# Pinning sixteen small loads in GpSimd's queue, in a two-layer graph network kernel

## The chip, the cores and the metric

The kernel runs on one core of one Trainium2 chip. The time is device microseconds of one launch. The core has five engines with a queue each: TensorE (PE in the profile, its weight loads PEld), VectorE (DVE), ScalarE (ACT), GpSimd (POOL) and SyncE (SP). GpSimd, SyncE and ScalarE also issue DMA transfers from their queues; the transfers themselves are done by 16 DMA engines that all queues share.

## What is computed

Two graph layers with residuals and layer norms over 4096 nodes with 512 features, with a dense 4096 x 4096 adjacency matrix. Cut to what matters:

```python
# layer 0
xw  = (x > 0) @ sign(L0_gnn_weight).T
x   = layernorm(x + relu(adj @ xw))
# layer 1
node_att = softmax(x @ node_w, axis=0)
h   = x @ edge_w
e   = where(adj > 0, h @ h.T, NEG_BIG)
out = (adj * node_att * softmax(e, axis=1)) @ (x @ weight) + bias
x   = layernorm(x + out)
```

The case is about layer 0's second half: the product with `adj`, and what is prepared there for layer 1.

## The kernel before

**Layer 0.** x and its products are cut into 32 blocks of 128 rows. For each block the kernel multiplies 32 tiles of 128 x 128 of the transposed adjacency matrix with `xw`, which lies in SBUF. To keep float32 accuracy[...], each adjacency tile is split into `hi` (a rounded copy, ScalarE, line 413) and `lo` (the rest, VectorE, line 415), and each part has its own matmul (lines 423 and 424). The split works in quarters of a block: eight tiles at a time, with two buffers each for `hi` and `lo`. A quarter is 16 matmuls, some 3.6 us of TensorE. The adjacency tiles (`at`) come through SyncE's queue, half a block a load, in three buffers. The first two rows of blocks (`early`) are multiplied while `xw` is still being made, so that after that stage the finishing work of two blocks comes at once.

**What follows a block.** `rest` is a Python generator, and one piece of it runs in each quarter of the blocks that follow, so that its instructions are spread between the splits:

- a first piece adds the residual and takes the row statistics (lines 320 to 322);
- a second normalises (line 326), and with `tensor_tensor_reduce` into the scratch tile `scr` takes the block's share of the node attention (line 327);
- a third adds the bias into `scr` (line 331) and stores it to `x1_d` in DRAM through GpSimd's queue (line 332). `scr` has one buffer;
- a fourth calls `left` after every second block, and starts `lefts` for some;
- a fifth transposes the block on TensorE (line 383), and `lefts` goes on in the pieces after it.

**Left operands for later.** The big products of layer 1 use a scheme with seven products instead of eight (Strassen's, in Winograd's form). Its left operands are sums and differences of pairs of blocks, and `left` makes them here: lines 371 to 374 on VectorE into `sums_l`, and four stores to `lop_d` in DRAM, all through GpSimd's queue (lines 375 to 378). For three of the seven operands the scheme is applied a second time within the operand. `lefts` makes these inner combinations, for the last two of every four pairs of blocks (eight times in all). It loads three pieces of an earlier pair's operands back from `lop_d` into the tile `low` with two loads (line 352), waits three pieces, and combines them with the present pair (lines 358 to 361: four operations of 128 x 128 for one operand, four of 128 x 256 for the other two). It stores the results to `lop2_d` (lines 363 and 364). `low` has one buffer.

**What else is in GpSimd's queue.** `premask` turns pieces of the adjacency matrix into masks for layer 1 (line 303 on VectorE), and stores them through GpSimd's queue (line 304). So in this stage the queue holds x1_d stores, lop_d stores, the `low` loads, lop2_d stores and mask stores, and a waiting instruction holds up all behind it.

**What sets the order.** The layer-0 loop runs under `tc.manual_schedule` for VectorE and ScalarE: their instructions keep the order of the program text. Those of GpSimd's queue do not: the scheduler of the language orders them by its own priorities and by when operands and buffers are ready in its reckoning. A DMA that reads what another wrote waits for that one's landing, and a load into `low` waits until the tile is free. `tc.keep_in_program_order(...)` around an instruction fixes its place among the instructions of its engine; `premask` uses it already for its conversion at line 303. The last block's `lefts` does not run in the loop: it is kept in `late` and goes on between the products of `hT`, the first product of layer 1 (line 101), where no manual schedule holds.

Of the kernel before, what the change touches and what calls it, by code (L numbers as in the profile page):

```python
# [29 lines left out]
def kernel(  # L30
# [13 lines left out]
    nc = tc.nc  # L44
# [114 lines left out]
    with (  # L159
# [153 lines left out]
        def rest(n, b, xb, acc, before):  # L313
# [3 lines left out]
            rstd = small.tile([P, 1], F32, name="rstd")  # L317
            scr = wp.tile([P, D], F32, name="scr", tag="scr")
            inner = n % 2 and n // 2 % BG > 1 and lefts(n // 2, xb)
            nc.vector.scalar_tensor_tensor(xb, acc, 0.0, xb, ALU.max, ALU.add)  # L320
            nc.vector.bn_stats(stats, xb)
# [25 lines left out]
        def lefts(b, high):  # L347

            to, of = lop2_d[b // BG][:, :, b % BG - 2], lop_d[b // BG][:, :, b % BG - 2, :]
            low = wp.tile([P, len(SPLIT), HD], F32, name="low")  # L350
            for k, m in ((slice(2), slice(4, 7, 2)), (2, 3)):
                nc.gpsimd.dma_start(low[:, k, :], of[:, m, :])
            for _ in range(3):
                yield
            for k, a, to_a in ((2, high[:, HD:], sums_l[:, 0, :]), (slice(2), sums_l[:, 1:4:2, :], None)):
                to_a = a if to_a is None else to_a
                (l11, l21), (l12, l22), (s4, s1) = ((x[..., :P], x[..., P:]) for x in (low[:, k, :], a, to_a))
                nc.vector.tensor_add(s1, l22, l21)
                nc.vector.tensor_sub(l21, l11, l21)
                nc.vector.tensor_sub(l11, s1, l11)  # L360
                nc.vector.tensor_sub(s4, l12, l11)
                yield
                nc.gpsimd.dma_start(to[:, k, :2], to_a.rearrange("p (n f) -> p n f" if k == 2 else "p k (n f) -> p k n f", f=P))
            nc.gpsimd.dma_start(to[:, :, 2:], low.rearrange("p k (n f) -> p k n f", f=P))
# [1260 lines left out]
```

## Time and profile before

| | before |
|---|---|
| median of 3 runs | 1927.56 us (1927.24 to 1929.25) |
| the profiled execution's own time | 1931.16 us |
| its span | 1929.4 us |
| TensorE busy in the span | 1908.7 us |
| mean granted TensorE clock | 0.997 |
| DMA | 520.93 MB, mean 270 GB/s |
| layer 0 | to about 516 us |
| `hT` products | 516 to 613 us |
| layer 1's attention and output | from 613 us |

The profile is of one execution, with instructions, waits and DMA packets recorded. Lines of its views name an engine, the source line (L352 is line 352), the operation, what it writes and reads ("low<-lop_d"), and idle time of the engine before it with what ended that ("<-DMA lop_d<-xb": the landing of the transfer from `xb` to `lop_d`). A transfer issued by GpSimd shows there as DMA_DIRECT2D, and its length there is that of the issue alone; when it landed is told apart. In a line of busy times by stage stand the stretch, its length, the busy time of PE, PEld, DVE, ACT and POOL with their instructions, the granted TensorE clock, the busy share of the DMA engines, and GB/s.

### The profile page before, as it was taken

To read this page: it belongs to the slowest core of one execution; us is meant where nothing else is said; L and a number is where in the kernel's file an instruction comes from. 1 tells how busy PE (TensorE), PEld (TensorE's weight loads), DVE (VectorE), ACT (ScalarE), POOL (GpSimd) and SP (SyncE) were. 2 spreads that over 40 slices of the span, in tenths; PEclk is the share of its full clock that TensorE was granted. 3 is DMA by queue.
4 is the path that set the end of the run, shared out by engine and by line. 5 is a ranking of instruction groups with operands and counts; after the bars stand their busy time and mean duration, and the time that the engine had idled before them with its cause. 6 is when DMAs were issued, how large, how long until landed. Compare 5 with 4: busy or idle time off the path is not lost.

```text
span 1929.4 us, 20429 instructions
## 1 busy us (share of the span) xinstructions
PE 1908.7 (99%) x6816; PEld 1224.0 (63%) x6816; DVE 1436.1 (74%) x2113; ACT 1023.3 (53%) x1647; POOL 309.5 (16%) x449
## 2 busy tenths in 40 slices
PE   8999999999999999999999999999999999999998
PEld 6788888888744445444555556666666666656646
DVE  6577777776876467566754877898779988888847
ACT  5333333333211477566767666656676567657731
POOL 0123232232331111101110111111111111110100
PEclk9999999999999999999999999999999999999999
DMA  9789989899585479477874888878777877787731
GB/s 306 274 297 341 337 316 353 303 346 329 204 285 196 157 268 336 165 256 276 305 277 161 305 292 305 288 287 287 265 287 277 296 276 278 263 290 257 286 118 55
DMA packets 143913, 520.93 MB, mean 270 GB/s; under 512 B 15040, under 2 KB 15040, under 8 KB 136128
## 3 DMA queue, kind: packets, MB, share of 16 engines
q1 hardware_dynamic: 64368, 235.43, 36.1%
q0 software_dynamic: 67632, 248.54, 34.1%
q10 hardware_dynamic: 11808, 35.66, 5.0%
q8 instruction: 54, 0.88, 0.2%
q14 instruction: 51, 0.42, 0.1%
HBM read 397.93 MB, written 121.63 MB: 269 GB/s over the span
## 4 chain that ended last, share of the span: by engine, by line
PE 93%; DVE 3%; DMA 2%; ACT 1%; issue 0%; ACTq 0%; POOL 0%; DVEq 0%
PE bank L1186 36%; PE seven L779 15%; PE acc L424 11%; PE acc L423 11%; PE pe L706 5%; PE seven L101 5%; PE po L1336 4%; PE pt L668 3%; PE acc L236 1%; PE acc L235 1%; PE pt L383 1%; PE pw L213 1%; DMA lop<-lop_d 1%; PE bank L1336 0%; DVE slot L955 0%
## 5 line engine op out<-in xcount | busy, mean ns | idle before, releaser
L1186 PE MATMUL bank<-lent,lop 128*128 128x256 f32 (+1 forms) x1496 | 483.1, 473 | 0.1
L1186 PEld LDWEIGHTS bank<-lent,lop 128*128 128x128 f32 x1496 | 284.2, 190 | 166.9 <-issue 140.1
L424 PE MATMUL acc<-xw,lo 128*128 128x512 f32 x960 | 376.0, 392 | 4.6 <-DVE lo L415 4.5
L423 PE MATMUL acc<-xw,hi 128*128 128x512 f32 x960 | 377.8, 394 | 0.0
L1186 PE MATMUL bank<-slot,lop 128*128 128x512 f32 (+1 forms) x800 | 288.1, 506 | 3.1 <-DMA lop<-lop_d 2.3
L413 ACT CAST hi<-at 128x1024 fp32r<-128x1024 f32 x120 | 126.3, 1052 | 211.0 <-PE acc L423 152.5
L1186 PEld LDWEIGHTS bank<-slot,lop 128*128 128x128 f32 x800 | 152.6, 191 | 118.0 <-issue 104.0
L1197 ACT COPY over<-bank 128x512 f32<-128x512 f32 x200 | 116.1, 584 | 202.3 <-PE bank L1186 198.5
L424 PEld LDWEIGHTS acc<-xw,lo 128*128 128x128 f32 x960 | 181.2, 189 | 42.2 <-DVE lo L415 5.2
L423 PEld LDWEIGHTS acc<-xw,hi 128*128 128x128 f32 x960 | 181.1, 189 | 37.0
L415 DVE TENSOR_TENSOR lo<-at,hi 128x1024 fp32r<-128x1024 f32 x120 | 147.0, 1225 | 68.8 <-ACT hi L413 68.3
L706 PE MATMUL pe<-hT 128*128 128x512 f32 (+3 forms) x384 | 132.1, 486 | 0.0
L639 ACT ACTIVATE line<-line,nmax_c 128x512 f32<-128x512 f32 x160 | 114.8, 725 | 22.6 <-DVE nmax_c L630 22.3
L630 DVE CUSTOM_DVE_ANT_0 line<-lent,slot 128x512 f32<-128x512 bf16 x140 | 90.7, 689 | 47.6 <-ACT slot L716 26.7
L1348 DVE SCALAR_TENSOR_TENSOR xb<-po,f,xb 128x256 f32<-128x256 f32 x84 | 40.3, 481 | 73.6 <-PE po L1336 73.6
L706 PEld LDWEIGHTS pe<-hT 128*128 128x128 f32 x384 | 64.6, 191 | 41.3 <-issue 33.8
L779 PE MATMUL seven<-hT 128*128 128x512 f32 x192 | 89.8, 593 | 0.0
L955 DVE CUSTOM_DVE_ANT_1 lent<-lent,line 128x2048 f32<-128x2048 f32 x39 | 88.7, 2284 | 0.0
L1159 ACT COPY bank<-over 128x512 f32<-128x512 f32 x144 | 86.7, 603 | 0.0
L668 PEld LDWEIGHTS pt<-ident,lent 128*128 128x128 f32 x418 | 52.3, 141 | 52.1 <-issue 38.6
L669 ACT COPY slot<-pt 128x512 f32<-128x512 f32 (+3 forms) x123 | 68.4, 559 | 23.2 <-PE pt L668 23.2
L958 ACT ACTIVATE lent<-lent 128x2048 f32<-128x2048 f32 x39 | 74.9, 1919 | 8.5 <-DVE lent L955 8.2
(270 smaller groups left out, 2947.9 us busy)
## 6 DMA issues: line engine op xcount, KB each, us to landing
lop<-lop_d SPq DMA_DIRECT2D x154, 512.0 KB, 4.6
at<-in_adj_t_dram SPq DMA_DIRECT2D x60, 1024.0 KB, 7.3
slot<-in_adj_t_dram POOLq DMA_DIRECT2D x39, 1024.0 KB, 7.8
lent<-s_d POOLq DMA_DIRECT2D x38, 1024.0 KB, 7.9
s_d<-slot POOLq DMA_DIRECT2D x30, 1024.0 KB, 7.3
lent<-in_adj_t_dram POOLq DMA_DIRECT2D x25, 1024.0 KB, 8.0
lent<-in_adj_dram SPq DMA_DIRECT2D x48, 512.0 KB, 5.3
s_d<-lent POOLq DMA_DIRECT2D x48, 512.0 KB, 4.3
```

The source lines that it names most:

```text
L101: nc.tensor.matmul(banks[bank][q], lop(m, q)[k], rop(m)[k], start=(first and k == 0), stop=(k == K - 1), skip_group_check=not first,)
L413: nc.scalar.copy(hi, aq)
L415: nc.vector.tensor_sub(lo, aq, hi.bitcast(F32))
L423: nc.tensor.matmul(acc, hi[:, c, :], xw[:, kb, :], start=(kb == 0), stop=False)
L424: nc.tensor.matmul(acc, lo[:, c, :], xw[:, kb, :], start=False, stop=(kb == NB - 1))
L630: nc.vector.tensor_tensor_reduce(line, mask, src, -1.0, HUGE, ALU.add, ALU.min, accum_out=nmax_c[:, b, c : c + 1])
L639: nc.scalar.activation(line, line, AF.Exp, bias=nmax_c[:, b, c : c + 1], scale=-1.0, accum_out=sum_c[:, b, c : c + 1])
L668: nc.tensor.transpose(pt[:, j, :], src[:, ts(j, P)], ident)
L706: nc.tensor.matmul(pe[:, lo * P :], hT[:, k, ts(A * BG + i, P)], hT[:, k, (B * BG + lo) * P : (B + 1) * W], start=(k == 0), stop=(k == KD ...
L779: nc.tensor.matmul(ps, left[m][:, k, q, :], right[m][:, k, :], start=(first and k == 0), stop=(k == KD // 2 - 1), skip_group_check=not first,)
L1186: nc.tensor.matmul(ps, lop[:, k, :], rop[:, k, :], start=start, stop=(k == K - 1), skip_group_check=True)
L1197: nc.scalar.copy(self.to(), self.bank[:, : self.w])
```

## The change

The two loads into `low` are wrapped in `tc.keep_in_program_order`:

```diff
             to, of = lop2_d[b // BG][:, :, b % BG - 2], lop_d[b // BG][:, :, b % BG - 2, :]
             low = wp.tile([P, len(SPLIT), HD], F32, name="low")
             for k, m in ((slice(2), slice(4, 7, 2)), (2, 3)):
-                nc.gpsimd.dma_start(low[:, k, :], of[:, m, :])
+                tc.keep_in_program_order(nc.gpsimd.dma_start(low[:, k, :], of[:, m, :]))
             for _ in range(3):
                 yield
```

In the program text `lefts` starts right after `left`. So each pair of loads now stands in GpSimd's queue directly behind the stores of lines 378 and 377 of the same pair of blocks. Before, the loads of the first of each two `lefts` stood some dozens of instructions earlier, between the stores of blocks before, and those of the second stood right behind the first's last stores. A piece of the start of GpSimd's queue, before and after:

```
before                          after
L376 lop_d<-xb                  L376 lop_d<-xb
L352 low<-lop_d                 L332 x1_d<-scr
L332 x1_d<-scr                  L378 lop_d<-sums_l
L378 lop_d<-sums_l              L377 lop_d<-sums_l
L377 lop_d<-sums_l              L375 lop_d<-xb
L375 lop_d<-xb                  L332 x1_d<-scr
L352 low<-lop_d                 L304 mask_d<-pair
L332 x1_d<-scr                  L304 mask_d<-pair
```

The other engines' orders stay the same but for VectorE's at the start of the `hT` products: there line 463, which prepares a right operand, now comes ahead of the last block's combinations at lines 358 to 361. Some of the work that follows them there (lines 122, 123, 303, 501 and 507) changes places by one or a few instructions.

## The prediction

> **What bounds the kernel now.** I read the page's busy shares first, then the busy time by stage, then who waited for whom in layer 0, and last the chain of work that ended last, followed through the one place where TensorE stood still.
>
> From the page (busy us, share of the span, instructions), and the busy time of each engine in two stretches of layer 0:
>
> ```profile
> PE 1908.7 (99%) x6816; PEld 1224.0 (63%) x6816; DVE 1436.1 (74%) x2113; ACT 1023.3 (53%) x1647; POOL 309.5 (16%) x449
> ...
> 60.00:100.00 40.00, 35.46 (x153) 28.88 (x152) 24.43 (x42) 11.91 (x17) 7.94 (x12) 0.91 0.71 240
> 100.00:500.00 400.00, 400.00 (x1815) 331.12 (x1814) 293.47 (x474) 129.92 (x159) 117.90 (x166) 1.00 0.90 328
> ```
>
> TensorE bounds the kernel. In 100 to 500 us, the bulk of layer 0, it is busy for all 400 us: whatever GpSimd waits for there costs nothing. Only 60 to 100 us has a hole, of 4.5 us, and a granted clock of 0.91. So the change can gain only there, and can lose anywhere. The waits of layer 0 (60 to 560 us: total us, times, longest):
>
> ```profile
> POOL low L352 <- DMA lop_d<-sums_l: 22.1, 4, 6.6
> POOL low L352 <- DMA lop_d<-low: 19.2, 4, 5.8
> POOL low L352 <- DMA lop_d<-xb: 13.8, 2, 7.2
> POOL low L352 <- issue: 13.7, 2, 7.1
> DVE scr L327 <- DMA x_d<-scr: 6.4, 3, 5.5
> PE acc L424 <- DVE lo L415: 4.5, 1, 4.5
> ```
>
> The 16 loads at L352 hold GpSimd's queue for 22.1 + 19.2 + 13.8 + 13.7 = 68.8 us in 12 waits. One of them, in the chain (start us, us, what), reaches TensorE:
>
> ```profile
> 69.02 7.71 DMA lop_d<-xb
> ...
> 77.00 0.57 POOL low L352
> 77.57 6.56 DMA x_d<-scr
> ...
> 84.96 1.15 DVE lo L415
> ...
> 86.15 0.79 PE acc L424
> 86.94 0.43 PE acc L423
> ```
>
> The load waited until the store of its own source had landed. The store x1_d<-scr, queued behind it, was held from 72.6 us (its L331 ended at 72.33; other such stores start 0.3 us after theirs) to 77.57. `scr` has one buffer, so VectorE's next L327 waited for that store, and the split `lo` stands behind L327. The timelines of VectorE and TensorE there (start, us, engine, instruction, idle before it and releaser):
>
> ```profile
> 78.17 0.55 DVE L326 TENSOR_SCALAR xb<-xb,mv,rstd 128x512 f32<-128x512 f32 x1
> 84.26 0.69 DVE L327 CUSTOM_DVE_ANT_0 scr<-xb,nw_b 128x512 f32<-128x512 f32 x1 [5.54 <-DMA x_d<-scr]
> ...
> 81.14 0.47 PE L423 MATMUL acc<-xw,hi 128*128 128x512 f32 x1
> 86.15 0.79 PE L424 MATMUL acc<-xw,lo 128*128 128x512 f32 x1 [4.54 <-DVE lo L415]
> 86.74 0.63 PE L423 MATMUL acc<-xw,hi 128*128 128x512 f32 x1
> ...
> 91.32 0.40 PE L424 MATMUL acc<-xw,lo 128*128 128x512 f32 x1
> ```
>
> [...] at 77.57 us the held store starts the moment the load has issued. [...] lop_d<-xb landed at 69.02 + 7.71 = 76.73 us, the load started at 77.00. [...] After the 4.54 us hole the records show 0.43 us from matmul to matmul, against 0.227 before it.
>
> **The change, part by part.** No instruction is added or removed: 16 loads move in GpSimd's queue, some of VectorE's work at the very end of layer 0 with them (4), and nothing on TensorE, ScalarE or SyncE. Before, the scheduler pulled them ahead. Pinned, each pair stands behind the L378 and L377 of its own block, where the source text has it.
>
> (1) The load at 77.00 goes from in front of the x1_d store. The store then issues at about 72.65. TensorE's loss, from 81.14 to 91.32 us: 10.18 us for 13 matmul steps, which at full pace take 0.32 (the step behind four transposes, as from 73.39 to 73.71) + 12 x 0.227 = 3.04. So 7.1 us: 4.7 of idleness and 2.4 of slow clock.
>
> What is late next? L327 could start at 78.75, when L326 is done. The store must land by then, 6.1 us after its issue. The 32 stores at L332 took 2.3 / 6.0 / 9.9 us (least, median, most). The one before it took 3.45, with spare DMA time: the share of the DMA engines is 0.25 to 0.36 in 74 to 78 us. It comes out of the queue behind lop_d<-xb (76.7), so I put it at 77 to 78. L327 (0.69) and `lo` (1.23) then end at 80.65, and TensorE wants `lo` at 81.46. The cover is 0.8 us: the store may take 6.9 us for nothing. At 9.9 it would land at 82.55 and leave 3.0 us of hole, most of it with the slow clock. The next loads of `at`, issued at 68.1 and 76.5, landed by 82.1, before the casts that want them even 7 us earlier. I take the full 7.1.
>
> (2) The other 11 waits of GpSimd go, 61 us of its queue. They are worth 0: TensorE has no hole in 100 to 500 us, and VectorE's other two waits for the store (0.26 and 0.59 us) reach nobody.
>
> (3) The loads come later, and VectorE's L358 may now wait for them. In the steady rhythm (block 2, times from L374 at 136.81) L378 issues 0.26 later and takes 1.02, L377 0.55, the pair 0.72 and 0.57. So the second load issues at +2.55, and L358 wants it at 146.96, which is +10.15: 7.6 us later.
>
> ```profile
> 146.96 0.29 DVE L358 TENSOR_TENSOR sums_l<-xb,low 128x128 f32<-128x128 f32 x1
> ...
> 149.40 1.23 DVE L415 TENSOR_TENSOR lo<-at,hi 128x1024 fp32r<-128x1024 f32 x1
> ```
>
> Behind L358 stand L359 to L361, L331, a mask conversion and this `lo`, which ends at 150.63; TensorE takes it up at 152.20. The slack is 1.57 us. So the load is free up to 9.15 us after its issue. Nearest rows: the loads themselves, 2.7 / 6.5 / 8.3 us, and L304, which holds that place in the queue now, in the loaded stretch of 400 to 430 us 7.9 / 8.4 / 11.0. [...] From above, 11.0 would be 1.85 us of TensorE in each of the 7 blocks inside the loop. I take 0, since both the median and the largest load fit.
>
> (4) The last block (15) is combined while layer 1's hT products run. Its loads now issue behind L377, which ended at 525.10: the second at about 525.8. Loads there took 2.7 to 3.1 us, so it lands near 529 instead of 520.6. VectorE's order changes with it: L463 is put ahead of L358. Eight small combinations (4 x 0.29 + 4 x 0.42 = 2.8 us) and L122 (0.69) then end near 532.6, and TensorE wants that bank at 533.91. It costs nothing with 1.3 us of cover; a landing of 8.3 us would cost about 4. GpSimd's reduction at L500 and the mask stores behind it shift by 1.3 us, with over 4 us before VectorE's use of the mask piece that waits for them (it landed at 540.8, used at 546.80).
>
> Sum against the profiled execution: 1931.16 (span 1929.4, 1.8 around it) - 7.1 = 1924.1. The runs' median lies 3.6 below the profiled execution, and I carry the saving over: 1927.56 - 7.1 = 1920.5.
>
> **Rivals.** A measurement of this kernel can tell 0.2%, 3.9 us, from no change.
> A, the full gain, 0.70: 1920.5. [...] DMA chance later in the kernel (a single 2.3 us wait for a lop load at 1719 us, with its own slow clock) adds about a microsecond each way: 1918.5 to 1922.5.
> B, the x1_d store still lands late, 0.12: at 8 to 9 us from issue 1.1 to 2.1 us of hole remain, some with slow clock, about 1924. For it: half the stores take over 6.0. Against: the idle DMA engines at 74 to 78 us.
> C, nothing gained, 0.08: the hole reopens at another wait behind it, 1927.5. Against: the chain shows no other wait within 4 us of that path.
> D, slower, 0.10: L358 waits for the pinned loads, with `lo` behind it. It decides from 9.15 us of landing, and must come to over 11 us to outweigh the gain by 3.9: 10.7 us at all 7 blocks. At 11.0 it is 7 x 1.85 = 13 us, 1927.56 - 7.1 + 13 = 1933.5. For it: DMA share 0.90 in this stretch and one L304 at 11.0. Against: no load over 8.3.
>
> The range takes in A and B, and leaves out C and D, 0.18: 1918.5 to 1926. Faster by over 0.2% is A and half of B: 0.76. Within it, the other half and C: 0.14. Slower: D, 0.10.
>
> **What would show it.** Right: L352 never starts after a DMA it waited for, L327's 5.54 us is gone, TensorE is full in 60 to 100 us with clock 1.00, and 100 to 500 stays at 400.00. Wrong: idle before L358 on "DMA low<-lop_d" over 1.6 us, a hole before L424 anywhere, or idle TensorE at 530 to 540 us.

## The result, and the profile after

| | before | after |
|---|---|---|
| median | 1927.88 us (6 runs, 1927.24 to 1929.82) | 1921.53 us (6 runs, 1920.88 to 1923.42) |
| profiled execution's own time | 1931.16 us | 1922.03 us |
| its span | 1929.4 us | 1920.3 us |
| first matmul at L423 to first `hT` matmul (L101) | 457.48 us | 450.33 us |

The ratio is 0.9966, 95% interval 0.9953 to 0.9979. That is 6.4 us faster, where 1920.5 us (7.1 us faster) was predicted. The prediction's mechanism held, and so did its steps, but for one wait of L358 that it left out and that cost nothing here. The page's busy line and the busy times of two stretches of layer 0, of the kernel after (columns as before):

```profile
PE 1904.1 (99%) x6816; PEld 1220.4 (64%) x6816; DVE 1437.1 (75%) x2113; ACT 1023.4 (53%) x1647; POOL 310.6 (16%) x449
...
60.00:100.00 40.00, 40.00 (x183) 33.08 (x182) 30.18 (x52) 13.98 (x19) 8.71 (x14) 1.00 0.83 290
100.00:500.00 400.00, 400.00 (x1816) 330.80 (x1815) 294.89 (x475) 130.88 (x161) 120.71 (x168) 1.00 0.89 325
```

TensorE now has 40.00 of 40 us in 60 to 100 us, 183 matmuls instead of 153, at clock 1.00 instead of 0.91. The bulk of layer 0 stays full. GpSimd's and VectorE's waits in 60 to 560 us:

```profile
POOL lop_d L376 <- DVE xb L326: 94.1, 15, 7.7
...
POOL x_d L332 <- DVE scr L331: 54.0, 25, 2.9
...
POOL lop_d L378 <- DVE sums_l L373: 41.0, 14, 4.7
...
DVE sums_l L358 <- DMA low<-lop_d: 0.5, 1, 0.5
```

No wait of L352 for another transfer is left, and none of L327. GpSimd's idle time has moved to waits for VectorE's results, which its stores need (before, the first three came to 83.7, 33.4 and 27.9 us). The place where the hole was, on GpSimd, VectorE and TensorE (timelines of the kernel after):

```profile
72.55 0.57 POOL L332 DMA_DIRECT2D x_d<-scr  x1 [2.87 <-DVE scr L331]
77.81 0.76 POOL L378 DMA_DIRECT2D lop_d<-sums_l  x1 [4.70 <-DVE sums_l L373]
```

```profile
78.09 0.72 DVE L326 TENSOR_SCALAR xb<-xb,mv,rstd 128x512 f32<-128x512 f32 x1
78.84 0.69 DVE L327 CUSTOM_DVE_ANT_0 scr<-xb,nw_b 128x512 f32<-128x512 f32 x1
79.45 0.08 DVE L327 DVE_READ_ACCUMULATOR2_ANT node_s<- 128x1 f32 x1
79.45 1.22 DVE L415 TENSOR_TENSOR lo<-at,hi 128x1024 fp32r<-128x1024 f32 x1
```

```profile
81.06 0.47 PE L423 MATMUL acc<-xw,hi 128*128 128x512 f32 x1
81.37 0.39 PE L424 MATMUL acc<-xw,lo 128*128 128x512 f32 x1
```

The x1_d store issues at 72.55, 0.29 us after its L331 ended. It landed at 77.61. L327 follows L326 without a wait, `lo` ends at 80.67, and TensorE takes it at 81.37 without a gap.

When both executions' matmuls are paired one by one, the kernel after is level with the one before up to 81 us, 4.78 us ahead at the end of the old hole, and 7.12 us ahead eleven matmuls on. It is 7.23 us ahead at the first `hT` matmul, and 7.21 at the 1801st matmul of L1186 (1703.83 against 1696.63 us). The spans differ by 9.1 us; the remaining 1.9 us come mostly from one late wait, for a `lop` load, which differs from profile to profile: 0.8 to 2.3 us in five of the seven, at most 0.13 us in the other two (TensorE's timeline, of before and of after):

```profile
1719.21 3.64 PE L1186 MATMUL bank<-slot,lop 128*128 128x256 f32 x8 [2.31 <-DMA lop<-lop_d]
```

```profile
1710.95 2.29 PE L1186 MATMUL bank<-slot,lop 128*128 128x256 f32 x8 [1.25 <-DMA lop<-lop_d]
```

The gap is 1.06 us longer before, and the eight matmuls behind it take 1.35 us more, at the slow clock (0.50 granted from 1719.34 to 1722.74 us); the wait for L967 that follows is 0.5 us shorter before, which leaves 1.06 + 1.35 - 0.5 = 1.9. The instructions there are the same in both kernels.

### The profile page after: what moved, and what is told of

It is laid out like the page before. It is cut to its first block, busy times and chain, and to the rows that moved or that the text cites. A ratio compares the mean times of both kernels' runs of the same rounds, so it can differ in the third digit from the quotient of the medians.

```text
span 1920.3 us, 20431 instructions
## 1 busy us (share of the span) xinstructions
PE 1904.1 (99%) x6816; PEld 1220.4 (64%) x6816; DVE 1437.1 (75%) x2113; ACT 1023.4 (53%) x1647; POOL 310.6 (16%) x449
## 4 chain that ended last, share of the span: by engine, by line
PE 89%; DVE 6%; ACT 2%; DMA 1%; issue 1%; ACTq 0%; DVEq 0%
PE bank L1186 33%; PE seven L779 14%; PE acc L424 11%; PE acc L423 11%; PE pe L706 5%; PE seven L101 5%; PE po L1336 4%; PE pt L668 2%; DMA lent<-in_adj_t_dram 1%; DVE slot L955 1%; PE pt L383 1%; PE acc L236 1%; PE acc L235 1%; PE pw L213 1%; PE bank L1336 0%
## 5 line engine op out<-in xcount | busy, mean ns | idle before, releaser
L1186 PE MATMUL bank<-lent,lop 128*128 128x256 f32 (+1 forms) x1496 | 483.0, 473 | 0.1
L1186 PEld LDWEIGHTS bank<-lent,lop 128*128 128x128 f32 x1496 | 283.8, 190 | 166.9 <-issue 140.1
L423 PE MATMUL acc<-xw,hi 128*128 128x512 f32 x960 | 376.4, 392 | 0.0
L1186 PE MATMUL bank<-slot,lop 128*128 128x512 f32 (+1 forms) x800 | 286.6, 503 | 2.6 <-DMA lop<-lop_d 1.3
L1186 PEld LDWEIGHTS bank<-slot,lop 128*128 128x128 f32 x800 | 151.4, 190 | 117.6 <-issue 102.5
L423 PEld LDWEIGHTS acc<-xw,hi 128*128 128x128 f32 x960 | 180.2, 188 | 36.7
```

Source lines behind the costliest of these rows:

```text
L423: nc.tensor.matmul(acc, hi[:, c, :], xw[:, kb, :], start=(kb == 0), stop=False)
L1186: nc.tensor.matmul(ps, lop[:, k, :], rop[:, k, :], start=start, stop=(k == K - 1), skip_group_check=True)
```

## The experiments

The theory: of the 12 waits at L352, one reaches TensorE, through the held store and the one `scr` buffer; the other waits and the later loads are worth nothing. The rivals: the gain is a sum over all the queue waits that go; or the store delays TensorE in another way than through `scr`; or the pinned loads, now late, take something back.

| kernel | median us (range) | runs | ratio to before (95% interval) | L423 to L101, us |
|---|---|---|---|---|
| first pair pinned | 1921.67 (1920.42 to 1924.64) | 5 | 0.9968 (0.9955 to 0.9980) | 450.04 |
| all but the first pair | 1928.13 (1926.56 to 1931.23) | 13 | 1.0002 (0.9994 to 1.0010) | 457.68 |
| `scr` freed for L327 | 1922.21 (1921.91 to 1923.34) | 6 | 0.9969 (0.9957 to 0.9981) | 451.45 |
| combinations earlier | 1937.90 (1933.91 to 1942.88) | 4 | 1.0052 (1.0034 to 1.0069) | 463.11 |
| combinations earlier, loads early | 1927.11 (1925.86 to 1929.95) | 12 | 0.9996 (0.9987 to 1.0004) | 455.70 |

The last column is of the profiled execution alone. The first four rows share the runs of the kernel before (19, median 1927.95); the last has 15 of its own (1927.77).

**The first pair alone, and all but it.** The kernel before with one pair of loads pinned, and its counterpart:

```diff
-                nc.gpsimd.dma_start(low[:, k, :], of[:, m, :])
+                (tc.keep_in_program_order if b == 2 else (lambda i: i))(nc.gpsimd.dma_start(low[:, k, :], of[:, m, :]))
```

```diff
-                tc.keep_in_program_order(nc.gpsimd.dma_start(low[:, k, :], of[:, m, :]))
+                (tc.keep_in_program_order if b != 2 else (lambda i: i))(nc.gpsimd.dma_start(low[:, k, :], of[:, m, :]))
```

> The kernel before, with only the first pair of the 16 low loads (b == 2) kept in its place in GpSimd's queue. The other 14 stay where the kernel before has them, so GpSimd still waits some 50 us for landings behind which its queue stands. Theory (one wait reaches TensorE, the one at 77.00 us): all of layer 0's gain, 7.1 us, so about 1920.8 us (1919.5 to 1922.5), with TensorE busy 40.00 in 60 to 100 us at clock 1.00, and some ten waits of L352 for lop_d left in the trace. Rival (the gain is the sum of many small ones, from the 69 us of queue waits that all go): one pair of 16 brings only its share, about 1 us, so 1926 to 1928.

> The counterpart: the kernel after, with only the first pair of low loads (b == 2) left where the kernel before had it; the other 14 loads are kept in place. Theory (one wait): no gain. VectorE's L327 waits again about 5.5 us for the x1_d store, TensorE has a hole of about 4.5 us at 81.6 to 86.2 us and then steps of 0.43 us[...]; about 1927.7 us (1926 to 1929). Rival (many small gains): most of it stays, about 1921 to 1923.

One pair, two of the 16 loads, brings the whole gain; the other 14 bring nothing. Stages and waits of the kernel with only the first pair pinned:

```profile
60.00:100.00 40.00, 40.00 (x183) 33.10 (x183) 30.18 (x52) 13.97 (x19) 8.67 (x14) 1.00 0.84 291
100.00:500.00 400.00, 400.00 (x1817) 331.05 (x1816) 294.46 (x475) 130.77 (x161) 122.86 (x168) 1.00 0.89 325
```

```profile
POOL low L352 <- DMA lop_d<-low: 20.3, 4, 6.3
POOL low L352 <- DMA lop_d<-sums_l: 16.7, 3, 6.0
POOL low L352 <- issue: 13.9, 2, 7.4
POOL low L352 <- DMA lop_d<-xb: 6.2, 1, 6.2
```

GpSimd still stands 20.3 + 16.7 + 13.9 + 6.2 = 57.1 us at L352, in ten waits, and TensorE is as full as in the kernel after. The pair took two of the twelve waits with it. That the one at 77.00 us mattered, and not the second, of 6.1 us at 86.16, is read from the chain of the kernel before, where TensorE has no gap behind the second in layer 0; no kernel pinned one load alone. In the counterpart the hole is back. VectorE's and TensorE's timelines there:

```profile
83.70 0.69 DVE L327 CUSTOM_DVE_ANT_0 scr<-xb,nw_b 128x512 f32<-128x512 f32 x1 [5.37 <-DMA x_d<-scr]
```

```profile
85.60 0.79 PE L424 MATMUL acc<-xw,lo 128*128 128x512 f32 x1 [4.37 <-DVE lo L415]
```

The rival, that the gain is a sum of many small ones, falls. The counterpart tells one thing more: 14 late loads, the last block's among them, cost at most 0.1% (the end of its interval).

**`scr` freed for L327.** All loads where the kernel before has them; in the first four blocks the throwaway product goes into a PSUM bank, out of the accumulators' pool, instead of `scr`:

```diff
-            scr = wp.tile([P, D], F32, name="scr", tag="scr")
+            scr = wp.tile([P, D], F32, name="scr", tag="scr"); junk = ps_mm.tile([P, D], F32, name="junk", tag="mm") if n < 4 else scr
...
-                scr, xb, nw_b, 1.0, 0.0, ALU.mult, ALU.add, accum_out=node_s[:, b : b + 1]
+                junk, xb, nw_b, 1.0, 0.0, ALU.mult, ALU.add, accum_out=node_s[:, b : b + 1]
```

> The kernel before with all loads where they were; in the first four blocks the throwaway product of L327 goes into a PSUM bank instead of scr, so that L327 no longer waits for the x1_d store. Nothing is left out. GpSimd's load still waits about 7 us at 77.00 and still holds the store of x1_d to 77.6, landing at about 84. Theory (the chain is load, held store, one scr buffer, L327, lo, TensorE): the wait of L327 goes, lo ends at about 80.7 in time for 81.46; L331, which also writes scr, then waits till about 84 with the next lo behind it, so that a smaller hole of 0 to 2 us comes near 85 us in place of 4.5. TensorE in 60 to 100 us: 38 to 40 of 40. Gain 4 to 7 us, 1920.5 to 1924. Rival (the late store itself, or GpSimd's queue behind it, holds TensorE some other way than through scr): hole as before, about 1927.5.

GpSimd's queue is held as before, VectorE's path is not. Timelines of this kernel, GpSimd, VectorE and TensorE:

```profile
76.78 0.58 POOL L352 DMA_DIRECT2D low<-lop_d  x1 [6.98 <-DMA lop_d<-xb]
77.36 0.54 POOL L332 DMA_DIRECT2D x_d<-scr  x1
```

```profile
78.96 0.70 DVE L327 CUSTOM_DVE_ANT_0 junk<-xb,nw_b 128x512 f32<-128x512 f32 x1
...
79.57 1.22 DVE L415 TENSOR_TENSOR lo<-at,hi 128x1024 fp32r<-128x1024 f32 x1
84.14 0.69 DVE L331 TENSOR_TENSOR scr<-xb,bias_b 128x512 f32<-128x512 f32 x1 [3.35 <-DMA x_d<-scr]
84.75 0.68 DVE L303 TENSOR_SCALAR pair<-pair 128x1024 bf16<-128x1024 f32 x1
85.35 1.22 DVE L415 TENSOR_TENSOR lo<-at,hi 128x1024 fp32r<-128x1024 f32 x1
```

```profile
86.63 0.50 PE L424 MATMUL acc<-xw,lo 128*128 128x512 f32 x1 [0.87 <-DVE lo L415]
```

The load waits 6.98 us and the store issues only at 77.36, as late as before. Yet the hole of 4.5 us is gone. The wait has moved to L331, the next writer of `scr`, where it leaves a hole of 0.87 us without a slow clock behind it (the matmuls from 86.96 us on step by 0.23 us). Against the kernel after this one loses 1.1 us in layer 0 (451.45 against 450.33 us), all of it at that matmul. So the late store reaches TensorE through `scr` and VectorE's order, as the chain said, and a queue wait as long as before (6.98 us) costs only the 1.1 us that `scr` still passes on. It is a second remedy for the same hole, 1.1 us poorer.

**Combinations earlier.** To see what a late load costs, its cover is taken away in the kernel after:

```diff
-            for _ in range(3):
+            for _ in range(2):
                 yield
```

> The kernel after with the combinations L358 to L361 one quarter of a block (some 3.5 us) earlier after their loads: two pieces between the loads and their use instead of three. This takes away the cover that I reckoned for the pinned loads (second load free up to 9.15 us after its issue; it landed 6.1 to 7.8 after it). Theory (a late L358 reaches TensorE through L359 to L361 and lo, one for one beyond the slack): the second load is due about 4 to 5 us after issue, so L358 waits 1.5 to 3.5 us in each of the 7 blocks inside the loop, and TensorE has holes of 0 to 2.5 us there, some with the slow clock: 1925 to 1940 us, about 1931. Rival (VectorE has more slack than reckoned, the loads don't come near TensorE): the waits stand in the trace but TensorE stays full in 100 to 500 us, 1921.5.

VectorE's waits in 60 to 560 us, and its timeline at the longest of them, with TensorE's:

```profile
DVE sums_l L358 <- DMA low<-lop_d: 12.6, 8, 2.9
```

```profile
261.83 0.29 DVE L358 TENSOR_TENSOR sums_l<-xb,low 128x128 f32<-128x128 f32 x1 [2.86 <-DMA low<-lop_d]
...
263.79 0.69 DVE L327 CUSTOM_DVE_ANT_0 scr<-xb,nw_b 128x512 f32<-128x512 f32 x1
264.41 0.08 DVE L327 DVE_READ_ACCUMULATOR2_ANT node_s<- 128x1 f32 x1
264.41 1.22 DVE L415 TENSOR_TENSOR lo<-at,hi 128x1024 fp32r<-128x1024 f32 x1
```

```profile
265.68 0.50 PE L424 MATMUL acc<-xw,lo 128*128 128x512 f32 x1 [2.04 <-DVE lo L415]
...
267.76 0.63 PE L423 MATMUL acc<-xw,hi 128*128 128x512 f32 x1
268.18 0.63 PE L424 MATMUL acc<-xw,lo 128*128 128x512 f32 x1
```

Every pair of loads is now waited for. The seven waits inside the loop come to 12.1 us, from 0.3 to 2.9 us each. Layer 0 becomes 463.11 - 450.33 = 12.8 us longer than in the kernel after. Of this 1.6 us is slow clock behind the one hole of 2.04 us (the eleven steps from 266.72 to 270.82 us took 4.10 us; at 0.227 each they are 2.50); the other 11.2 us stand against 12.1 us of waits, nearly one for one. The forecast's waits (1.5 to 3.5 us each) held for five of the seven; the median is near the upper end of what was expected. The profiled execution was the fastest of the four, so the others lost more than it shows; where they lost it is not on record.

**Its control.** But this edit also moves L358 to L361 into other quarters of VectorE's work, so the loss may be theirs. The same edit, with only the first pair of loads pinned and the others early:

> Control for the run before it: the same earlier combinations (two pieces between loads and use, so the same order on VectorE, TensorE and ScalarE), but only the first pair of low loads is kept in place; the other 14 are issued early, as in the kernel before. Theory (the loss of that run is VectorE waiting for loads issued late): of its eight waits for the loads only the first pair's stays, with a hole of about 0.9 us near 142 us, and TensorE is otherwise full in 100 to 500 us: about 1922.5 (1921 to 1925). Rival (the earlier combinations themselves crowd their quarter of VectorE, whatever the loads do): holes and loss as in that run, 1934 to 1943.

Neither forecast was met: 1927.11 us lies between 1922.5 and 1934. The hole near 142 us came as expected (1.0 us at 142.54), but smaller ones followed in other blocks. VectorE's waits, and its timeline at one of them:

```profile
DVE sums_l L358 <- DMA lop_d<-sums_l: 5.2, 5, 1.4
...
DVE sums_l L358 <- DMA low<-lop_d: 1.8, 1, 1.8
```

```profile
380.80 0.29 DVE L358 TENSOR_TENSOR sums_l<-xb,low 128x128 f32<-128x128 f32 x1 [0.84 <-DMA lop_d<-sums_l]
```

Seven of the eight waits for loads are gone, as the theory had it, but five of them had another wait close beneath. L358 writes into `sums_l`, from which L378 and L377 have just been stored, so it also waits for those stores to land. At 380.80 the load had landed 50 us earlier, the stores at 380.78. Layer 0 is 5.4 us longer than in the kernel after: 1.8 of waiting for the one pinned pair and 4.0 for stores inside the loop, less 0.5 of slack. What remains of the loss of the run before, 463.11 - 455.70 = 7.4 us in the profiles and 10.8 us between the medians, goes with the late loads, the only difference between the two kernels. That the earlier combinations cost nothing by themselves, as was expected, is false. That it is the stores rests on this trace (L358 starts 0.02 to 0.09 us after they land, four times in the loop); no kernel without that wait was run.

## Why the prediction was right

**The bound.** Right. Only 60 to 100 us could gain, and the 7.2 us arose there.

**(1) The hole.** Each link came within 0.1 us of the working, or inside its range:

| | predicted | measured |
|---|---|---|
| x1_d store issues | 72.65 | 72.55 |
| it lands | 77 to 78 | 77.61 |
| L327 starts | 78.75 | 78.84 |
| `lo` ends | 80.65 | 80.67 |
| TensorE wants `lo` | 81.46 | 81.37 |
| layer 0 gains | 7.1 | 7.2 |

The store took 5.1 us, and the reason given for 77 to 78 us held too: in all four kernels that pin this pair and leave `scr` as it was, the store took 4.4 to 5.1 us and landed 0.62 us after the store `lop_d<-xb` queued ahead of it. Rival B, a store that lands late again, needed more than 6.9 us. C, a hole that opens again behind another wait, is out too: no gap of TensorE follows in layer 0.

**(2) The other waits are worth nothing.** Right, and shown by the two kernels that pin the first pair or all but it.

**(3) The loads come later.** In GpSimd's order the first pair of each two moved back by 18 to 25 instructions (not the "some dozens" of the section on the change), the second by 4 to 6. The cost of 0 was right, and so was the landing: 2.7 / 6.5 / 8.3 us was taken, and the source view of the kernel after has at L352

```profile
DMA to landing us min/median/max: 3.1/6.6/8.1
```

The cover was less ample than the medians suggest. The slowest second load took 7.75 us (issued at 252.00), and L358 waited 0.13 us for it, out of 1.57 us of slack behind L358. Rival D's mechanism is real: the run with the earlier combinations shows a late L358 reaching TensorE nearly one for one, at 12.8 us over the layer. It did not occur because no load took over 9.15 us (8.1 at most).

What the working left out is L358's other wait, for the stores from `sums_l`. The kernel before already had it: its store at 407.85 landed at 416.15 us and L358 began at 416.72, with 0.57 us to spare. The pinned loads land 0.8 to 1.5 us behind those stores. So the change does not put a new kind of risk on L358; it moves a limit that was there by about 1 us. With that seen, D could have been bounded by the stores in the trace of before, which stand right in front of the loads' new place, and not by L304 and the loads at their old places.

**(4) The last block.** Right. Its second load issues at 518.58 and lands at 521.67, which is 525.8 and 528.9 on the old time axis (525.8 and 529 predicted). L358 waits 0.52 us for it, instead of 1.12 for a store before, and TensorE has no gap.

**The sum.** The prediction lies 1.0 us under the median. The cause term is not to blame: 7.1 was taken, 7.2 measured. What is left is in the carrying over. The kernel before came out 0.3 us higher in six runs than in the three at hand, and the medians differ by 6.4 us instead of 7.2. The interval of the ratio, 0.9953 to 0.9979, is 4.0 to 9.1 us, so these runs do not tell 6.4 from 7.2. The stretch from the 1801st matmul of L1186 to the end, the same instructions in all seven kernels, took 222.0 to 225.6 us in the seven profiled executions. That alone is more than the difference. Of A's range, 1918.5 to 1922.5 us, about a microsecond each way was for DMA chance; the rest was the author's estimate, which no trace showed.

## What to carry to other kernels

A wait in a queue costs what stands behind it, not its own length: of 69 us of waiting at one line, 7 us of queue time held one store, that store held a single-buffered tile, and the rest was free. So follow each wait to the engine that sets the end before giving it a price, and change the one that arrives there. When transfers are moved later, look for every wait of the instruction that uses them, also for stores that must leave the tile it overwrites: the nearest of these says how much room the new order has.

## What the runs showed of the hardware

- In these runs the longer holes of TensorE cost more than the hole, and the shorter ones did not:

  | kernel | hole, us | its end, us | the matmuls behind it |
  |---|---|---|---|
  | before | 4.54 | 86.15 | steps of 0.43 us from 86.74 to 91.01, against 0.227 before the hole; granted clock 0.50 from 84.35 to 91.17 us |
  | all but the first pair | 4.37 | 85.60 | steps of 0.43 us from 86.19 to 91.31 |
  | before | 2.31 | 1719.21 | eight of L1186 (128x256) took 3.64 us; granted clock 0.50 from 1719.34 to 1722.74 us |
  | combinations earlier | 2.04 | 265.68 | steps of 0.43 us from 267.33 to 270.32 |
  | combinations earlier, loads early | 1.96 | 1731.86 | eight of L1186 (128x512) took 5.40 us |
  | after | 1.25 | 1710.95 | eight of L1186 (128x256) took 2.29 us; granted clock 1.00 in 1709 to 1713 us |
  | after | 1.13 | 1726.42 | eight of L1186 (128x512) took 3.70 us; granted clock 1.00 in 1715 to 1730 us |
  | `scr` freed | 0.87 | 86.63 | steps of 0.23 us from 86.96 on |

- In the kernel after, the second pinned load, 128 KB, took 6.1 to 7.8 us from issue to landing in six blocks between 130 and 410 us, where the DMA engines were busy 0.91 of the time, and 3.1 us in the last two, at 494 and 519 us (share 0.60 in 490 to 510 us and 0.33 in 510 to 530).
